# Two pre-activation conv blocks on one core: three engines keep the written plan's order in the front loop and the first convolution

## The chip, the cores and the metric

The program runs on 1 core of a Trainium2 chip. The metric is the device time of one launch in microseconds; before the change it is 4217.51 us, the median of 3 runs (4216.18 to 4220.4). The profiled run has a span of 4215.7 us, and the times below are counted from that span's start.

## The reference, cut to what matters

x is (4, 64, 256, 256) in fp32. `_gn` is a group norm with 32 groups of two channels, without scale. Two layers follow each other:

```python
# layer 0
h = gelu(conv3x3(gn(x), c1_w) + c1_b);  xa, k = split(conv1x1(h, c2_w) + c2_b)
xs = gelu(depthwise 3x1 (depthwise 1x3 (xa)))
mask = top 2 of 3 softmax gate weights of mean(xs)         # over the whole image
y = x + conv1x1(xs + sum_i expert_i(k, xs) * mask_i, proj_w)
# layer 1
h1 = conv3x3(gn(y), q(w1)) + b1;   h1 = relu(batchnorm(h1))  # over all 4 images
h2 = conv3x3(h1, q(w2)) + b2;      out = y + relu(batchnorm(h2) + gn(y))
```

Three things have to be known before work on them can start: the group norm of an image of x before its first convolution, the gate of an image before its experts' output (it needs the last row of xs), and the batch norm of all h1 before the second convolution.

## The kernel before, in words

Partitions hold two times 64 channels: two rows of the image stand side by side, so an image is 128 row pairs of 256 columns. A *group* is two row pairs (512 columns, one PSUM bank); there are 64 of them (NG). A *chunk* is 4 groups (1 MB for DMA); an image has 16 (NCH). A *step* of the front loop does two groups of an image: 32 steps per image (NOCT), 128 for the four images.

The stages are:

- Statistics of image 0 of x: 16 chunks are loaded (stats_load, L268) and run through bn_stats on VectorE (stats_group, L277).
- The front loop (layer 0). Per step it does, on TensorE, the first convolution c in two parts (L396 and L402, matmuls recorded at L328, Gelu on ScalarE L407), the taps a in two parts (L438 and L444; ScalarE L450, two VectorE passes L451 and L454, edge fix L457, Gelu with sum L469), the projection p of two groups (L490), whose result VectorE adds onto x in place (L493), and every second step the expert products k (L476) and q (L506; VectorE L509). After a chunk's last projection SyncE stores it as t1 to DRAM (L495 in the profile). Once an image's gate is known, out_groups adds the experts' part o (L570) to t1, read back by out_load (L559), takes bn_stats of y (L575, L576) and stores y (L581). This runs inside the next image's front loop, 1.25 pairs of groups per step. Inside the front loop of images 0, 1 and 2 stand also the statistics of the next image of x.
- The first convolution of layer 1 (conv1): 65 steps per image. conv1_load (L597) reads a chunk of y, conv1_prepare normalises it on ScalarE (L604), rounds it into the *upper* half tile (ScalarE, L258) and takes the rest as the *lower* half (VectorE, L259). Each group is then 12 matmuls (L247), an eviction by ScalarE (L619) and bn_stats (L624). The out_groups of image 3 run in its first 128 steps.
- A second convolution with the batch norm folded into its input (L768 on), and an output stage that is a stream of loads and stores.

**Buffers.** The ring `in` holds 3 chunks: x of the front loop, later y of conv1. front_load of chunk k therefore waits until chunk k−3 has been stored as t1. The tag `s` holds 2 chunks of the statistics' x (later h1), the tag `o` 3 chunks of y. PSUM has two banks each for c, a and o, one for p and one for k.

**GpSimd** pads the loaded x with the group's mean (front_pad, L363), and writes a one-column *tick* (L321) between the groups of quarter-array matmuls and the full-array matmul that divides them: the next quarter matmuls wait for the tick. A tick queued behind a padding waits for that padding's x.

**What sets the order.** The calls are written into a plan, `plan[step, order]`, and carried out in sorted order (L705 to L707). front_load of chunk k stands at step 2k−1 of its image, order 0. The proj that ends chunk k−3 stands at step 2k−2, order 7. Carrying out the plan doesn't fix the instructions' order on their engines: the framework's scheduler takes the recorded instructions and orders each engine's queue by its own estimate of readiness; an engine then runs its queue in order. Ties in one (step, order) go by insertion.

Of the kernel before, what the change touches and what calls it, by code (L numbers as in the profile page):

```python
# [9 lines left out]
F32 = mybir.dt.float32  # L10
F32R = mybir.dt.float32r
AF = mybir.ActivationFunctionType
ALU = mybir.AluOpType
# [25 lines left out]
CG = 4  # L39
CPAIR = CG * GP  # L40
# [11 lines left out]
def conv_preact_kernel(ctx: ExitStack, tc: tile.TileContext, io, col128, colset, col64):  # L52
    nc = tc.nc
# [36 lines left out]
    def split_tiles(pool, name):  # L90

        tiles = [
            [pool.tile([P, CPAIR + 1, PW], F32R, name=f"half_{name}{i}{j}", bufs=1) for j in range(2)]
            for i in range(2)
        ]
        for t in (*tiles[0], *tiles[1]):
            nc.gpsimd.memset(t.bitcast(F32)[:, :, 0 : PW : PW - 1], 0.0)
        return tiles

    halves = split_tiles(layers.enter_context(tc.tile_pool(name="halves1", bufs=1)), "1")  # L100
# [8 lines left out]
    plan = defaultdict(list)  # L109

    def at(step, order, call, *args):
        plan[step, order].append((call, args))
# [139 lines left out]
                stop=(j == len(terms) - 1),  # L252
            )

    def prepare(halves, y, k, a=0, e=CPAIR + 1):

        upper, lower = (t[:, a:e, 1 : 1 + W] for t in halves[k % 2])
        nc.scalar.activation(upper, y[:, a:e, :], AF.Copy)  # L258
        nc.vector.tensor_tensor(lower, y[:, a:e, :], upper.bitcast(F32), ALU.subtract)  # L259

    gn1, gn2, c1s, c1_bias = {}, {}, {}, {}
    bn1 = const.tile([P, B, 2], F32, name="bn1")
# [329 lines left out]
    y_in, h_out, st_h = {}, {}, {}  # L592
# [4 lines left out]
        nc.sync.dma_start(y[:, a : CPAIR + 1, :], y_d[b][:, k * CPAIR + a - 1 : (k + 1) * CPAIR, :])  # L597

    def conv1_prepare(b, k):
        y = y_in.pop((b, k))  # L600
        a = 1 if k == 0 else 0
        if k == 0:
            nc.gpsimd.memset(y[:, 0, :], 0.0)
        nc.scalar.activation(y[:, a:, :], y[:, a:, :], AF.Identity, bias=gn2[b][:, 2:3], scale=gn2[b][:, 1:2])  # L604
        prepare(halves, y, k)

    def conv1(b, s):

# [43 lines left out]
    def plan_front(b):  # L652
        t = b * F_STEPS
        for k in range(NCH):
            if b > 0 or k >= 2:
                at(t + 2 * k - 1, 0, front_load, b, k)
                at(t + 2 * k - 1, 1, front_pad, b, k)
        for n in range(NOCT):
            at(t + n, 2, front_conv_a, b, n)
            at(t + n, 5, front_conv_b, b, n)  # L660
            at(t + n + 2, 6, front_taps_a, b, n)
            at(t + n + 2, 9, front_taps_b, b, n)
            at(t + n + 3, 3, front_proj, b, n, 0)
            at(t + n + 3, 7, front_proj, b, n, 1)
        for j in range(NG // 4):
            at(t + 2 * j + 3, 4, front_k, b, j)
            at(t + 2 * j + 4, 8, front_q, b, j)
        if b == 0:
            for n in range(3):
                at(n, 3, front_divide, b, n)  # L670
                at(n, 7, front_divide, b, n)
        at(t + NOCT + 2, 1, gate, b)

    def plan_stats(b, t, per):

        for k in range(NCH):
            at(t + int((k - 1) * CG / per), 0, stats_load, b, k, "s", 2)
        for g in range(NG):
            at(t + int(g / per), 10, stats_group, b, g)
        at(t + int(NG / per) + 1, 10, stats_end, b)  # L680

    def plan_out(b, t, per, order):

        for k in range(NCH):
            at(t + int((k - 1.5) * 2 / per) - 1, 0, out_load, b, k)
        for j in range(NG // 2):
            at(t + int(j / per), order, out_groups, b, j)
        at(t + int(NG / 2 / per) + 1, 10, out_end, b)

    def plan_conv1(b):  # L690
        t = CONV1 + b * (NG + 1)
        for k in range(NCH):

            at(CONV1 - 1 + 2 * k if b == 0 and k < 3 else t + 4 * k - 9, 0, conv1_load, b, k)
            at(t + (-1, 2)[k] if b == 0 and k < 2 else t + 4 * k - 4, 1, conv1_prepare, b, k)
        for s in range(NG + 1):
            at(t + s, 2, conv1, b, s)

    for b in range(B):
        plan_front(b)  # L700
        if b < B - 1:
            plan_stats(b + 1, b * F_STEPS + 2, 2.35)
        plan_out(b, (b + 1) * F_STEPS + 3, 1.25 if b < B - 1 else 0.25, 4)
        plan_conv1(b)
    for key in sorted(plan):  # L705
        for call, args in plan[key]:
            call(*args)  # L707


    def bn_affine(mv, gamma, beta, out, name):  # L710
# [16 lines left out]
    def conv2_prepare(i):  # L727
        b, k = chunks[i]
        h = h_in.pop(i)

        cuts = (0, GP + 1, CPAIR + 1) if i == 0 else (0, CPAIR + 1)
        for a, e in zip(cuts, cuts[1:]):
            nc.scalar.activation(h[:, a:e, :], h[:, a:e, :], AF.Relu, bias=ss1[:, 1:2], scale=ss1[:, 0:1])
            if k == 0 and a == 0:
                nc.gpsimd.memset(h[C:P, 0, :], 0.0)
            if k == NCH - 1:
                nc.gpsimd.memset(h[0:C, CPAIR, :], 0.0)
            prepare(halves2, h, k, a, e)
# [62 lines left out]
    for i, (b, k) in enumerate(steps):  # L801
        if i + AHEAD < len(steps):
            end_load(i + AHEAD)
        y, h = y_of.pop(i), h2.pop((b, k))
# [122 lines left out]
```

## Time and profile before

| stretch, us | what | TensorE busy, us | DMA share | GB/s |
|---|---|---|---|---|
| 60 to 89 | weights, start of image 0 | 17.07 of 29 | 0.82 | 251 |
| 89 to 610 | front loop, image 0 | 457.43 of 521 | 0.49 | 151 |
| 610 to 1149 | front loop, image 1 | 517.55 of 539 | 0.48 | 129 |
| 1149 to 1685 | front loop, image 2 | 516.71 of 536 | 0.49 | 130 |
| 1685 to 2220 | front loop, image 3 | 517.27 of 535 | 0.48 | 130 |
| 2220 to 2279 | hand-over to conv1 | 48.29 of 59 | 0.39 | 141 |
| 2279 to 3020 | conv1 | 737.17 of 741 | 0.64 | 228 |
| 3020 to 3750 | second convolution | 720.44 of 730 | 0.48 | 180 |
| 3750 to 4216 | output | 1.18 of 466 | 1.00 | 389 |

The images' limits are the ends of their last Gelu evictions (L407). Over the whole span TensorE is busy 3533.1 us (84%), VectorE 2157.8 us (51%), ScalarE 1667.8 us (40%), GpSimd 58.8 us. A busy time of TensorE counts overlapping quarter-array matmuls once, so it tells where the engine stood still, not how full its array was. A row of a timeline gives start, length, engine (SPq is SyncE issuing DMAs), line, operation, output and inputs, how many were merged into the row, and in brackets the idle time before it and what ended it.

### The profile page before, as it was taken

To read this page: it belongs to the slowest core of one execution; us is meant where nothing else is said; L and a number is where in the kernel's file an instruction comes from. 1 tells how busy PE (TensorE), PEld (TensorE's weight loads), DVE (VectorE), ACT (ScalarE), POOL (GpSimd) and SP (SyncE) were. 2 spreads that over 40 slices of the span, in tenths; PEclk is the share of its full clock that TensorE was granted. 3 is DMA by queue.
4 is the path that set the end of the run, shared out by engine and by line. 5 is a ranking of instruction groups with operands and counts; after the bars stand their busy time and mean duration, and the time that the engine had idled before them with its cause. 6 is when DMAs were issued, how large, how long until landed. Compare 5 with 4: busy or idle time off the path is not lost.

```text
span 4215.7 us, 52658 instructions
## 1 busy us (share of the span) xinstructions
PE 3533.1 (84%) x21596; PEld 1829.6 (43%) x21596; DVE 2157.8 (51%) x2909; ACT 1667.8 (40%) x1962; POOL 58.8 (1%) x359
## 2 busy tenths in 40 slices
PE   3679999999999999999998999999999999950000
PEld 1223333333333332333335777788788888840000
DVE  7753334444444454444545665544444444466566
ACT  0123332222322223322225555666566666642222
POOL 0000000000000000000000000000000000000000
PEclk9889999999999999999999999999999999975555
DMA  9772324554335553354545777555455555349999
GB/s 309 270 222 74 78 78 114 147 147 135 103 104 151 147 154 105 104 144 127 157 128 183 266 260 248 202 201 202 171 202 201 199 204 191 122 163 413 412 412 393
DMA packets 351968, 805.79 MB, mean 191 GB/s; under 512 B 19120, under 2 KB 289456, under 8 KB 289776
## 3 DMA queue, kind: packets, MB, share of 16 engines
q1 hardware_dynamic: 334736, 682.36, 50.2%
q10 hardware_dynamic: 16992, 120.07, 7.2%
q8 instruction: 170, 2.79, 0.3%
q14 instruction: 70, 0.57, 0.0%
HBM read 480.97 MB, written 321.39 MB: 190 GB/s over the span
## 4 chain that ended last, share of the span: by engine, by line
PE 51%; DMA 8%; SPq 4%; DVE 4%; ACT 3%; issue 1%; POOL 0%; ACTq 0%; POOLq 0%; DVEq 0%
PE ps_h L247 30%; PE ps_c L328 10%; DMA y_end<-y_d 4%; PE ps_a L328 4%; PE ps_p L490 3%; SPq L815 3%; PE ps_o L570 2%; DMA yn<-y_d 2%; DMA x<-in_x 1%; SPq L810 1%; PE ps_k L476 1%; DVE half L259 1%; ACT v L806 1%; DVE h L807 1%; ACT half L258 1%; ACT yn L604 1%
## 5 line engine op out<-in xcount | busy, mean ns | idle before, releaser
L247 PE MATMUL ps_h<-half,w_q 128*128 128x512 f32 x6168 | 1450.3, 396 | 6.6 <-ACT half L258 4.7
L247 PEld LDWEIGHTS ps_h<-half,w_q 128*128 128x128 f32 x6168 | 1160.2, 189 | 308.9 <-issue 18.7
L328 PE MATMUL ps_c<-x,c1s 64*64 64x512 f32 x9216 | 1091.6, 607 | 2.0 <-POOL x L363 1.4
L328 PEld LDWEIGHTS ps_c<-x,c1s 64*64 64x64 f32 x9216 | 349.6, 135 | 697.0 <-issue 670.9
L493 DVE TENSOR_TENSOR x<-ps_p,x 128x512 f32<-128x512 f32 x256 | 177.0, 691 | 803.2 <-PE ps_p L490 778.8
L328 PE MATMUL ps_a<-h,av 64*64 64x512 f32 (+1 forms) x3568 | 388.1, 543 | 34.1 <-POOL tick L321 34.0
L490 PE MATMUL ps_p<-xs,m 128*128 128x512 f32 x512 | 296.8, 662 | 70.0 <-ACT xs L469 68.4
L450 ACT ACTIVATE t<-ps_a,tap_bias,m 128x512 f32<-128x512 f32 x256 | 185.1, 773 | 430.4 <-PE ps_a L328 430.4
L407 ACT ACTIVATE h<-ps_c,c1b 128x512 f32<-128x512 f32 x256 | 161.8, 683 | 473.3 <-PE ps_c L328 473.3
L771 DVE BATCH_NORM_STATS2 st_h<-h 128x6 f32<-128x512 f32 x256 | 173.8, 690 | 238.8 <-ACT h L770 238.8
L469 ACT ACTIVATE xs<-t 128x512 f32<-128x512 f32 x256 | 161.2, 630 | 322.6 <-DVE t L457 291.2
L451 DVE SCALAR_TENSOR_TENSOR t<-ps_a,m,t 128x510 f32<-128x510 f32 x256 | 189.9, 743 | 176.2 <-ACT t L450 176.2
L328 PEld LDWEIGHTS ps_a<-h,av 64*64 64x64 f32 x3568 | 140.8, 133 | 300.2 <-issue 198.6
L770 ACT ACTIVATE h<-ps_h,m,scale_w 128x512 f32<-128x512 f32 x256 | 196.9, 769 | 180.5 <-PE ps_h L247 178.6
L619 ACT ACTIVATE h<-ps_h,m,scale_w 128x512 f32<-128x512 f32 x256 | 195.8, 771 | 168.1 <-PE ps_h L247 162.6
L624 DVE BATCH_NORM_STATS2 st_h<-h 128x6 f32<-128x512 f32 x252 | 169.0, 688 | 179.9 <-ACT h L619 179.7
L806 ACT ACTIVATE v<-y_end,shift,gn 128x2048 f32<-128x2048 f32 x64 | 133.8, 2092 | 314.6 <-DMA y_end<-y_d 308.0
L259 DVE TENSOR_TENSOR half<-h,half 128x2304 fp32r<-128x2304 f32 (+1 forms) x65 | 163.8, 2520 | 147.8 <-ACT half L258 147.8
L259 DVE TENSOR_TENSOR half<-yn,half 128x2304 fp32r<-128x2304 f32 x64 | 163.7, 2558 | 134.3 <-ACT half L258 134.1
L807 DVE SCALAR_TENSOR_TENSOR h<-h,ss,v 128x2048 f32<-128x2048 f32 x64 | 150.3, 2350 | 153.7 <-ACT v L806 150.7
L575 DVE SCALAR_TENSOR_TENSOR y<-ps_o,ob,y 128x512 f32<-128x512 f32 x256 | 186.7, 741 | 60.7 <-PE ps_o L570 60.7
L277 DVE BATCH_NORM_STATS2 st_x<-xs_in 128x6 f32<-128x512 f32 x256 | 159.9, 680 | 75.8 <-DMA xs_in<-in_x 75.3
(150 smaller groups left out, 2037.6 us busy)
## 6 DMA issues: line engine op xcount, KB each, us to landing
h_d<-h ACTq DMA_DIRECT2D x114, 1024.0 KB, 4.1
h<-h_d SPq DMA_DIRECT2D x64, 1152.0 KB, 5.2
yn<-y_d SPq DMA_DIRECT2D x60, 1152.0 KB, 5.5
xs_in<-in_x SPq DMA_DIRECT2D x64, 1024.0 KB, 5.0
t_d<-x SPq DMA_DIRECT2D x64, 1024.0 KB, 4.8
y<-t_d SPq DMA_DIRECT2D x64, 1024.0 KB, 6.0
y_d<-y SPq DMA_DIRECT2D x256, 256.0 KB, 4.0
y_end<-y_d SPq DMA_DIRECT2D x64, 1024.0 KB, 11.4
```

The costliest lines, as they stand in the source:

```text
L247: nc.tensor.matmul(ps[:, 0:n, :], w[:, kx, m, :], t[:, i + m : i + m + n, kx : kx + W], start=(j == 0), stop=(j == len(terms) - 1),)
L259: nc.vector.tensor_tensor(lower, y[:, a:e, :], upper.bitcast(F32), ALU.subtract)
L328: ins = nc.tensor.matmul(ps[o, at_out[0] : at_out[1], :], w[i], rhs[i], **flags)
L450: nc.scalar.activation(flat(t), flat(ps), AF.Identity, bias=tap_bias, scale=sh[:, 1:2])
L451: nc.vector.scalar_tensor_tensor(t[:, :, 1:W], ps[:, :, 0 : W - 1], sh[:, 0:1], t[:, :, 1:W], ALU.mult, ALU.add)
L490: divide(nc.tensor.matmul(flat(ps), c128("proj"), xss[b, g], start=True, stop=True))
L493: nc.vector.tensor_tensor(t1, ps, t1, ALU.add)
L575: nc.vector.scalar_tensor_tensor(y, ps, out_bias[b], y, ALU.add, ALU.add)
L619: nc.scalar.activation(h, ps, AF.Identity, bias=c128("b1"), scale=w_scale["w1"])
L770: nc.scalar.activation(o, ps, AF.Identity, bias=c128("b2"), scale=w_scale["w2"])
L806: nc.scalar.activation(v, y, AF.Identity, bias=shift[:, b : b + 1], scale=gn2[b][:, 1:2])
L807: nc.vector.scalar_tensor_tensor(h, h, ss2[:, 0:1], v, ALU.mult, ALU.add)
```

## The change

The plan's calls are carried out inside a manual schedule for three engines: SyncE (SP), VectorE (DVE) and GpSimd (Pool) keep the order in which the plan records their instructions. TensorE and ScalarE are still ordered by the scheduler. Since the plan's order now counts, some places in it are changed:

- front_pad goes from order 1 to order 6 of its step.
- stats_load goes from order 0 to order 11, the end of its step.
- out_load goes from order 0 to order 5, and starts at most two steps ahead of its stage.
- conv1's preparation is divided: normalising and the upper half (ScalarE) stay at order 1, the lower half (VectorE) goes to order 10.

It is for having each queue's order follow from the plan and not from the scheduler's estimate. No instruction is added or removed.

```diff
-    def prepare(halves, y, k, a=0, e=CPAIR + 1):
+    def prepare(halves, y, k, a=0, e=CPAIR + 1, do=("upper", "lower")):
         upper, lower = (t[:, a:e, 1 : 1 + W] for t in halves[k % 2])
-        nc.scalar.activation(upper, y[:, a:e, :], AF.Copy)
-        nc.vector.tensor_tensor(lower, y[:, a:e, :], upper.bitcast(F32), ALU.subtract)
+        if "upper" in do:
+            nc.scalar.activation(upper, y[:, a:e, :], AF.Copy)
+        if "lower" in do:
+            nc.vector.tensor_tensor(lower, y[:, a:e, :], upper.bitcast(F32), ALU.subtract)
...
     def conv1_prepare(b, k):
-        y = y_in.pop((b, k))
+        y = y_in[b, k]
...
-        prepare(halves, y, k)
+        prepare(halves, y, k, do=("upper",))
+
+    def conv1_lower(b, k):
+        prepare(halves, y_in.pop((b, k)), k, do=("lower",))
...
-                at(t + 2 * k - 1, 1, front_pad, b, k)
+                at(t + 2 * k - 1, 6, front_pad, b, k)
...
-            at(t + int((k - 1) * CG / per), 0, stats_load, b, k, "s", 2)
+            at(t + int((k - 1) * CG / per), 11, stats_load, b, k, "s", 2)
...
-            at(t + int((k - 1.5) * 2 / per) - 1, 0, out_load, b, k)
+            at(max(t + int((k - 1.5) * 2 / per) - 1, t - 2), 5, out_load, b, k)
...
             at(t + (-1, 2)[k] if b == 0 and k < 2 else t + 4 * k - 4, 1, conv1_prepare, b, k)
+            at(t + (-1, 2)[k] if b == 0 and k < 2 else t + 4 * k - 4, 10, conv1_lower, b, k)
...
-    for key in sorted(plan):
-        for call, args in plan[key]:
-            call(*args)
+
+    with tc.manual_schedule(
+        engines={mybir.EngineType.SP, mybir.EngineType.DVE, mybir.EngineType.Pool}
+    ):
+        for key in sorted(plan):
+            for call, args in plan[key]:
+                call(*args)
```

## The prediction

> **What bounds the kernel now.** I read the page's slices first, for the stage in which TensorE is not full.
>
> ```profile
> PE   3679999999999999999998999999999999950000
> DVE  7753334444444454444545665544444444466566
> DMA  9772324554335553354545777555455555349999
> GB/s 309 270 222 74 78 78 114 147 147 135 103 104 151 147 154 105 104 144 127 157 128 183 266 260 248 202 201 202 171 202 201 199 204 191 122 163 413 412 412 393
> ```
>
> A slice is 105 us. TensorE (PE) is full from slice 5 to slice 35, except in slices 1 to 3; there the DMA and VectorE (DVE) rows are at their front-loop highest. The last four slices are a DMA-bound tail that the change does not touch. So the stage to look at is the first image of the front loop. The table of windows gives it in numbers (columns: window, its length, then busy time and count of PE, PEld, DVE, ACT, POOL, granted clock, DMA share, GB/s):
>
> ```profile
> 130.00:272.00 142.00, 97.31 (x680) 29.93 (x680) 99.42 (x172) 26.19 (x50) 1.79 (x14) 0.82 0.78 268
> 330.00:562.00 232.00, 232.00 (x1906) 75.80 (x1902) 79.27 (x138) 73.71 (x140) 5.90 (x41) 1.00 0.32 80
> ```
>
> Same image, same work per step: 680 matmuls in 142 us against 1906 in 232 us, that is 4.8 and 8.2 per us. Who is waited for between 60 and 330 us stands in the table of waits (total, times, longest):
>
> ```profile
> DVE st_x L277 <- DMA xs_in<-in_x: 67.4, 25, 9.1
> ACT xs L469 <- DVE t L457: 71.3, 16, 10.2
> PE ps_p L490 <- ACT xs L469: 59.1, 8, 15.9
> POOL x L363 <- DMA x<-in_x: 54.7, 4, 16.2
> ```
>
> The chain is legible: VectorE sits in a bn_stats of the *next* images until its chunk lands, ScalarE waits for VectorE's t, TensorE waits for ScalarE. And the padding waits for the image's own x. SyncE's timeline says why x is late:
>
> ```profile
> 107.15 65.41 SPq L270 DMA_DIRECT2D xs_in<-in_x  x17
> 176.14 0.39 SPq L495 DMA_DIRECT2D t_d<-x  x1
> 177.35 0.34 SPq L270 DMA_DIRECT2D xs_in<-in_x  x1
> 181.41 2.61 SPq L355 DMA_DIRECT2D x<-in_x  x4
> ```
>
> The scheduler has put 17 statistics loads ahead of the first t1 store; all 48 MB of images 1 to 3 go through here.
>
> From the ends of the Gelu evictions (L407, trace) I take step lengths. Undisturbed, steps of image 0 alternate 12.7 and 15.6 us (k's matmuls in every second one). Steps 3 to 10 took 31.6, 21.4, 25.6, 21.7, 25.5, 21.9, 25.5, 18.5: against 15.6, 12.7, ... an excess of 78 us.
>
> Images 1 to 3 (539, 536, 535 us) lose time at single chunks of x:
>
> ```profile
> 1299.32 0.34 SPq L559 DMA_DIRECT2D y<-t_d  x1
> 1299.76 0.38 SPq L495 DMA_DIRECT2D t_d<-x  x1
> 1308.07 2.62 SPq L355 DMA_DIRECT2D x<-in_x  x4
> 1316.63 0.34 POOL L363 TENSOR_SCALAR x<-zeros,gn 128x20 f32<-128x20 f32 x1 [11.93 <-DMA x<-in_x]
> 1317.05 1.09 PE L328 MATMUL ps_a<-h,av 64*64 64x512 f32 x8 [3.12 <-POOL tick L321]
> 1317.96 7.03 PE L328 MATMUL ps_c<-x,c1s 64*64 64x512 f32 x48
> ```
>
> The chunk's buffer comes free when the t1 store lands. A y load 0.44 us ahead of it doubled that, to 8.2 us; x then lands 8.4 us after its first issue, the tick stands behind the padding on GpSimd, and TensorE stops 3.1 us. Such stalls cost 18 us in image 1, 15 in image 2 and 15 in image 3 (chunks 5, 9 and 13, some 5 us each).
>
> **What the skill says.** "TensorE: Matmul & The Clock Gate", section "Architectural detail": ACT and DVE are strict FIFO. The trace agrees: with bn_stats ahead, t waits up to 18.8 us for nothing of its own. "DMA: Bandwidth & Descriptors", section "Queues, rings and completion order": a queue's descriptors are consumed in ring order. The trace agrees: loads issued *behind* x leave it at 8.5 us (first issue 181.4, landed 189.9; undisturbed 8.4), and one ahead of the store costs 4 us. The clock-gate page, section "What's actually happening", has the array fall to half clock after an idle window of about 3.4 us; here the 48 matmuls after the 3.12 us gap took 7.03 us, 5.33 elsewhere, so I add up to 1.7 us to long stalls.
>
> **The change part by part.** The order of the built program tells what moves.
>
> *SyncE, image 0.* The 48 stats loads spread over images 0 to 2, one per 1.7 steps. Nothing then holds x or t: −78 us. That takes the steady part (232 of 232 us busy) as the pace, with its DMA at 80 GB/s and 32%: a stats load per 1.7 steps, about 25 us, adds 42 GB/s.
>
> *VectorE.* Each step gains 2 or 3 bn_stats of 0.68 us after t. In that place VectorE was idle 2.16 us before x (L493); three take 2.0. Hidden. Loads are issued one to two steps (13 to 30 us) ahead and land in 4.7 to 12 us, so no wait on arrival.
>
> *SyncE, the new waits.* In each of images 0 to 2, six stats loads stand between a t1 store and its x load (chunks 5, 6, 7, 11, 12, 13). For 7 and 13 the buffer is free: the load goes out at once behind the store; at 222.1 the same sequence left the store at 5.2 and x at 8.9 us. Cost 0. For 5, 6, 11 and 12 the buffer is freed by a bn_stats of the same step, executed after the t's: they end 5.3 us after the store's issue, plus 0.7. So SyncE holds until +6.2, x is issued at +6.9 instead of +4.5, and lands behind 1 MB in the ring (+0.8, estimated from pieces landing 1.25 us apart). Padding is done at +16.6; image 0 tolerates +14.6 (chunk 8: store 390.0, matmul 405.6, less 1.0 for the taps behind the tick). Late by 2.0, with some cold clock 2.8: 4 × 2.8 = +11 us in image 0. If every such wait were absorbed: 0; if all six paid 4 us: 24.
>
> *Images 1 to 3, y loads.* y chunks 6 and 11, and the next image's first, move away from the store of chunks 5, 9 and 13. In image 3, with no stats loads, all three stalls go: −14. In images 1 and 2 chunk 5 keeps half (late 1.2 + 1.5 instead of 5), 9 and 13 go (−4.5, −5), chunk 11 (tolerates +15.9) becomes late by 0.7 and costs 2, chunk 6 0.5: −9 each.
>
> *End of statistics.* In program order bn_aggr (1.86 us) comes after the step's t's, so TensorE's first small matmul, now after 18 records of c instead of before them, waits until about 6.3 us into the step; the scheduler had it early and hidden. Partly that replaces waits of 1.4 and 1.2 us. Estimate +2.5 for an x chain, +1.5 for a y chain: 3 × 2.5 + 3 × 1.5 = +12 (0 to 22).
>
> *Padding later.* GpSimd's built order differs by one instruction (chunk 2 of image 0). Cost 0: that padding's data is needed 50 us later.
>
> *First convolution.* There TensorE is busy 737 of 741 us, so nothing is to be gained. lower at the step's end: the upper copy ends 3.0 us into a chunk's last-but-four step, bn_stats and a y pair (2.9) end by 5.1, lower (2.56) by 7.7, needed at 11.2 (4 steps of 2.8). Hidden. Only the hand-over changes: lower of chunk 1 now stands behind the whole gate on VectorE. By hand from the trace (gate's last op 8 us after ps_g, then bn_stats, two x, low, lower: 6 us) TensorE stands about 12 us with four matmuls begun, but saves the 9.08 us that it waited for xs at 2236.6; chunk 2 then waits about 4 more: +7 (−3 to +20).
>
> Sum: −78 + 11 − 18 − 14 + 12 + 7 = −80; 4217.5 − 80 = 4138.
>
> **Rivals.** (a) *Everything absorbed*: no new stall, chain or hand-over cost, all stalls of images 1 to 3 gone (18 + 15 + 15): −126, 4091. For: ring slack of 6 to 7 us at half the chunks of images 1 to 3; against: 1.1 us in image 0. (b) *VectorE's order binds the first convolution*: lower misses its 11.2 us at the 32 chunks beside y work by 2 us: +64, 4202. Against: 3.5 us of margin; for: VectorE is 55% busy there and a late h shifts all behind it. (c) *SyncE's order becomes the bound*: a stats load that waits for VectorE holds the next t1 store or x load at every chunk, not at four. 48 chunks × 3.7 (2.0 + 1.7 cold) = 178, of which about 16 is counted: 4138 + 162 = 4300, slower. For: SyncE issues everything in one order and the slack is only 2 us; against: loads of odd steps stand *behind* x. (d) *The 78 us come back elsewhere*: the same 48 MB compete in images 0 to 2 and slow t1 and x by 1.7 us per chunk: 48 × 1.7 = 80, 4218, no change.
>
> **How the numbers follow.** Forecast 0.73 (4138, spread about 4105 to 4170), a 0.07, b 0.08, c 0.08, d 0.04. Faster: forecast, a, b = 0.88; same 0.04; slower 0.08. The range 4103 to 4195 takes in the unknown costs (new stalls 0 to 24 in image 0, chains 0 to 22, hand-over −3 to +20) and leaves out c, d, a and the far part of b.
>
> **What would show it.** Right: slices 1 to 3 at 9 on the PE row and near 100 GB/s, image 0 about 455 us long, a wait SPq L270 <- DVE st_x of some us at four chunks per image, stalls behind the tick at image 0's chunks 5, 6, 11 and 12, and no long PE gap at 2236. Wrong: tick waits at most chunks (c), waits of ps_h for lower in steady chunks (b), or image 0 short and images 1 and 2 longer by as much (d).

## The result, and the profile after

The changed kernel takes 4144.74 us (median of 4 runs, 4140.64 to 4146.6) against 4216.85 us for the kernel before beside it (4215.34 to 4220.4): a ratio of 0.9826, 95% interval 0.9809 to 0.9844. The profiled executions, 4144.1 and 4215.7 us, differ by 71.6 us; all the accounts below are of these two. The forecast was 4138 us, range 4103 to 4195: faster, as the result is, and 6.7 us too low.

The slices of the page, of the kernel after (one slice is 103.6 us), in the rows that were shown of before:

```profile
PE   3999999999899999999999999999999999950000
DVE  5434445656366564555546566444444444465656
DMA  7334446665366663455536776655455555359999
GB/s 233 100 103 116 107 120 182 182 182 156 95 183 186 193 168 94 127 147 153 141 95 239 256 256 239 224 202 196 183 194 201 202 200 196 113 183 412 412 413 394
```

TensorE is at 8 or 9 from slice 1 to slice 35: the dip to 6 and 7 in slices 1 and 2 is gone. In slices 1 to 3 the DMA moves 100, 103 and 116 GB/s where it moved 270, 222 and 74: the 48 MB of statistics chunks are spread. The table of windows of the kernel after, over the two stretches that were shown of before (window, length, busy time and count of PE, PEld, DVE, ACT, POOL, granted clock, DMA share, GB/s):

```profile
130.00:272.00 142.00, 136.38 (x1066) 43.42 (x1058) 59.64 (x101) 40.92 (x78) 3.12 (x23) 0.95 0.42 118
330.00:562.00 232.00, 221.06 (x1734) 71.75 (x1726) 96.61 (x167) 70.40 (x131) 7.23 (x39) 0.96 0.37 96
```

1066 matmuls in the first 142 us instead of 680: that is what was won. But the second stretch has 1734 instead of 1906 and is no longer full: something new stands there, and the end of image 0 (554 us, before 610) now lies in it too. The table of waits of TensorE between 60 and 2150 us of the kernel after names it (total, times, longest):

```profile
PE ps_a L330 <- POOL tick L323: 24.7, 15, 2.9
PE ps_m_x L222 <- DVE mv_x L238: 11.0, 3, 3.7
PE ps_m_y L222 <- DVE mv_y L238: 10.7, 3, 3.6
```

The 59 us of ps_p <- xs are gone. The tick's waits are the x loads that come late; the two ps_m rows, which were not there before, are the ends of the statistics. On SyncE the forecast's new wait, L272 <- st_x, is there too: 8 waits between 89 and 560 us, 129.6 us in all, 65.7 of it in one at the start.

From the ends of the Gelu evictions I take step lengths again and put each excess to its cause. "Stalls" are excesses at single chunks of x; the last row before the sum is what the other rows leave over.

| term of the forecast | forecast, us | measured, us |
|---|---|---|
| steps 3 to 10 of image 0 come down to 12.7 and 15.6 | −78 | −81 |
| new waits of SyncE, image 0 (chunks 5, 6, 7, 11, 12, 13) | +11 | +24.2 (5.8, 5.8, 0.6, 4.6, 5.9, 1.5) |
| stalls of images 1 to 3, old ones gone less new ones | −32 | −36.0 (−10.5, −11.2, −14.3) |
| ends of statistics | +12 | +20.1 (2.7, 9.3, 7.1, 1.0 in images 0 to 3) |
| hand-over and first convolution | +7 | +5.1 |
| start, single steps, tail | 0 | −4.0 |
| sum | −80 | −71.6 |

Here is chunk 5 of image 0 in the kernel after. First SyncE's timeline: t1 store, statistics load, x load.

```profile
194.78 0.38 SPq L497 DMA_DIRECT2D t_d<-x  x1
200.91 0.33 SPq L272 DMA_DIRECT2D xs_in<-in_x  x1
201.33 2.68 SPq L357 DMA_DIRECT2D x<-in_x  x4
```

The store lands at 199.6; SyncE holds the statistics load until 200.91, when a bn_stats has freed its buffer, and x goes out 6.5 us after the store (forecast 6.9). It lands at 211.7, 10.4 us after its first issue (forecast 9.3), and the padding is done 17.5 us after the store (forecast 16.6, tolerated 14.6). Then TensorE's timeline, at this chunk and at the undisturbed chunk 8:

```profile
212.41 1.98 PE L330 MATMUL ps_a<-h,av 64*64 64x512 f32 x8 [2.83 <-POOL tick L323]
214.17 7.39 PE L330 MATMUL ps_c<-x,c1s 64*64 64x512 f32 x48
...
306.67 1.09 PE L330 MATMUL ps_a<-h,av 64*64 64x512 f32 x8
307.58 5.33 PE L330 MATMUL ps_c<-x,c1s 64*64 64x512 f32 x48
```

TensorE stands 2.83 us, and the same 56 matmuls behind the gap take 2.95 us longer than at chunk 8 (0.89 + 2.06). Behind the gap TensorE runs cold, that is at half its granted clock, and here that costs as much as the wait itself.

An end of statistics, image 0, in the timelines of VectorE (first line) and TensorE of the kernel after:

```profile
535.78 1.88 DVE L238 BATCH_NORM_AGGREGATE mv_x<-st_x 128x2 f32<-128x384 f32 x1
...
531.40 2.74 PE L330 MATMUL ps_c<-x,c1s 64*64 64x512 f32 x18
537.80 0.56 PE L222 MATMUL ps_m_x<-mv_x,m 128*128 128x1 f32 x2 [3.66 <-DVE mv_x L238]
538.29 1.98 PE L330 MATMUL ps_c<-x,c1s 64*64 64x512 f32 x8
540.20 0.58 PE L230 MATMUL ps_v_x<-d_x,m 128*128 128x1 f32 x2
540.72 2.83 PE L330 MATMUL ps_c<-x,c1s 64*64 64x512 f32 x12
```

bn_aggr stands behind the step's t's; TensorE waits 3.66 us for it, and then again runs cold: 8 matmuls in 1.98 us, as many as take 1.09 warm (chunk 8 above), and 12 in 2.83, which take 1.93 at full clock in a kernel further down (bn_aggr ahead). With the small matmuls between them that is about 2.2 us more.

### The profile page after: what moved, and what is told of

Same layout as the page of the kernel before. It is cut to its first block, busy times and chain, and to the rows that moved or that the text cites. A ratio compares the mean times of both kernels' runs of the same rounds, so it can differ in the third digit from the quotient of the medians.

```text
span 4144.1 us, 52631 instructions
## 1 busy us (share of the span) xinstructions
PE 3522.8 (85%) x21596; PEld 1826.3 (44%) x21596; DVE 2186.9 (53%) x2909; ACT 1669.2 (40%) x1962; POOL 59.1 (1%) x359
## 4 chain that ended last, share of the span: by engine, by line
PE 75%; DMA 11%; DVE 6%; SPq 5%; ACT 2%; issue 1%; POOL 0%; POOLq 0%; ACTq 0%; DVEq 0%
PE ps_h L247 34%; PE ps_c L330 21%; PE ps_a L330 7%; PE ps_p L492 6%; DMA y_end<-y_d 4%; DMA x<-in_x 4%; PE ps_o L572 3%; SPq L825 2%; PE ps_k L478 2%; PE ps_q L508 1%; DMA t_d<-x 1%; DMA out<-h 1%; SPq L820 1%; DVE h L817 1%; SPq L357 1%
## 5 line engine op out<-in xcount | busy, mean ns | idle before, releaser
L330 PE MATMUL ps_a<-h,av 64*64 64x512 f32 (+1 forms) x3568 | 386.6, 540 | 24.8 <-POOL tick L323 24.7
L453 DVE SCALAR_TENSOR_TENSOR t<-ps_a,m,t 128x510 f32<-128x510 f32 x256 | 190.9, 746 | 213.2 <-ACT t L452 213.2
L456 DVE SCALAR_TENSOR_TENSOR t<-ps_a,m,t 128x510 f32<-128x510 f32 x256 | 191.7, 749 | 9.0
L578 DVE BATCH_NORM_STATS2 st_y<-y 128x6 f32<-128x512 f32 x256 | 177.8, 695 | 8.9
```

The costliest lines, as they stand in the source:

```text
L330: ins = nc.tensor.matmul(ps[o, at_out[0] : at_out[1], :], w[i], rhs[i], **flags)
L453: nc.vector.scalar_tensor_tensor(t[:, :, 1:W], ps[:, :, 0 : W - 1], sh[:, 0:1], t[:, :, 1:W], ALU.mult, ALU.add)
L456: nc.vector.scalar_tensor_tensor(t[:, :, 0 : W - 1], ps[:, :, 1:W], sh[:, 2:3], t[:, :, 0 : W - 1], ALU.mult, ALU.add)
L578: nc.vector.bn_stats(st_y[b][:, g, :], y)
```

## Experiments: which kept order it takes

Only the set of engines that keep the plan's order is changed.

```diff
-        engines={mybir.EngineType.SP, mybir.EngineType.DVE, mybir.EngineType.Pool}
+        engines={mybir.EngineType.SP}
```

> SyncE's queue alone keeps the plan's order; VectorE and GpSimd are ordered by the scheduler again. Theory (the queue's order is what freed image 0: with the 48 stats loads spread, no bn_stats can hold VectorE for long, whoever orders it): the steps 3 to 10 of image 0 are about 116 us together as in the changed kernel (before: 192), and the time is within 15 us of the changed kernel, 4130 to 4160 us. Rival (VectorE's order is needed, because the scheduler puts a bn_stats ahead of the step's t wherever it thinks the chunk has landed): waits of DVE bn_stats for loads come back and image 0 keeps 20 us or more of its excess, 4165 us or more.

Measured: 4219.51 us, ratio to the kernel before 1.0014 (1.0005 to 1.0022). The whole gain is gone, though not where the rival put it: image 0 lasts 455.6 us, shorter than in the changed kernel (466.4), and steps 3 to 10 are 113 us. Image 3 (518.5 against 521.7) and the hand-over with the first convolution (794.6 against 807.0) are shorter too. But images 1 and 2 grow to 586.8 and 577.0 us (538.2 and 530.6 in the changed kernel). The waits of VectorE, then of TensorE, of this kernel between 546 and 1710 us, which is images 1 and 2:

```profile
DVE st_x L279 <- DMA xs_in<-in_x: 149.8, 29, 10.8
...
PE ps_p L492 <- ACT xs L471: 39.2, 13, 7.7
PE ps_o L572 <- DVE y L577: 28.1, 16, 8.4
```

The scheduler puts bn_stats ahead of work that TensorE needs, and VectorE waits in it for a chunk that isn't there: up to 10.8 us. In image 0 it does that too (13 waits, 77.2 us in all) and TensorE hardly feels it; in images 1 and 2, where VectorE also has the y pairs, it does. There the trace has 27 gaps of TensorE of over 0.7 us, 93 us in all. Six are ends of statistics; each of the other 21, 85 us, has such a wait of VectorE less than 8 us ahead of it or beside it. Half clock behind the gaps costs another 51 us; in these images of the changed kernel it costs 15. The theory that SyncE's order is enough falls: spreading the loads over images 0 to 2 spreads the waits with them, unless VectorE's order puts bn_stats where its chunk has landed. The outcome is that of the forecast's rival (d), 78 us that come back elsewhere; the way is another, for (d) had t1 and x slowed by the traffic, and here it is VectorE's order.

```diff
-        engines={mybir.EngineType.SP, mybir.EngineType.DVE, mybir.EngineType.Pool}
+        engines={mybir.EngineType.DVE}
```

> VectorE alone keeps the plan's order; SyncE's queue is ordered by the scheduler. Theory (the two-buffer statistics tag can't run ahead of a VectorE that reads its chunks in the plan's order, so the loads are spread whoever orders the queue): image 0 loses its 78 us of excess here too, steps 3 to 10 about 116 us, and the time is 4130 to 4160 us; with y loads standing next to the t1 stores again, stalls of some 5 us at x chunks 5 and 9 of images 1 to 3 come back, which is up to 25 us of that. Rival (the queue's order is what matters): stats loads stand ahead of t1 stores and x loads again, image 0 is 500 us or longer, 4185 us or more.

Measured: 4201.26 us, ratio 0.9970 (0.9959 to 0.9981). Image 0 does as the theory says (459.2 us, steps 3 to 10 at 117 us): with VectorE in order the two-buffer tag spreads the loads by itself. But images 1 to 3 last 560.2, 560.0 and 537.7 us, together 67 us more than in the changed kernel, where the theory allowed 25; the time itself lies where the rival had it, above 4185. SyncE's timeline of this kernel at chunk 5 of image 0:

```profile
195.85 0.37 SPq L497 DMA_DIRECT2D t_d<-x  x1
201.18 0.60 SPq L357 DMA_DIRECT2D x<-in_x  x1
201.97 0.46 SPq L272 DMA_DIRECT2D xs_in<-in_x  x1
202.49 1.93 SPq L357 DMA_DIRECT2D x<-in_x  x3
```

The scheduler slips statistics loads between the four pieces of x; and in images 1 to 3 y loads stand 0.4 us ahead of t1 stores again (at chunk 5 of image 1 the store then lands after 9.3 us). Here the last piece of this x lands 13.2 us after the first was issued (214.4), against 8.4 undisturbed. In TensorE's waits of this kernel between 60 and 2150 us, the tick's row, 24.7 us in the changed kernel, has become

```profile
PE ps_a L330 <- POOL tick L323: 65.6, 22, 6.8
```

So SyncE alone gives nothing, VectorE alone 0.3%, both (with GpSimd) 1.7%. The two do different things: VectorE's order keeps bn_stats from holding the engine, SyncE's keeps the loads out of the way of t1 and x. GpSimd is not what the two kernels lack: in their traces its paddings and ticks follow each other as in the changed kernel, but for one padding of image 0.

For GpSimd the question is the padding's place.

```diff
-                at(t + 2 * k - 1, 6, front_pad, b, k)
+                at(t + 2 * k - 1, 1, front_pad, b, k)
```

> The changed kernel with the padding back at its old place in the step, which with GpSimd in the plan's order is one tick earlier. Theory (the place is needed for the kept order: the padding of a chunk then holds a tick for x; by the trace the tick at 298.5 us of the changed kernel would wait for the x that lands at 304.8, and TensorE has about 2 us to spare): each of 61 chunks costs some 4.5 us of wait and 1.7 us of cold clock, about +380 us, 4520 us (4350 to 4600). Rival (the tick has slack of a whole half step, so one place more or less costs nothing): within 10 us of 4145.

Measured: 4443.93 us, ratio 1.0537 (1.0520 to 1.0555): 300 us slower than the changed kernel. The timelines of GpSimd and TensorE of this kernel at one of the 61 chunks:

```profile
151.68 0.34 POOL L365 TENSOR_SCALAR x<-zeros,gn 128x20 f32<-128x20 f32 x1 [14.74 <-DMA x<-in_x]
151.94 0.10 POOL L323 MEMSET tick<- 128x1 f32 x1
...
152.10 5.15 PE L330 MATMUL ps_c<-x,c1s 64*64 64x512 f32 x24 [4.30 <-POOL tick L323]
```

One place earlier, and the padding waits 14.74 us for x with a tick behind it, for which TensorE stands 4.30 us and then takes 5.15 us for 24 matmuls (2.81 when warm). The theory is right in kind and 80 us too high in size (51 waits of ps_c for the tick in the front loop, not 61). The kernel before had its paddings behind that tick too, all but one as in the changed kernel, though the plan had them ahead of it; so against that kernel the later place costs nothing, as forecast. Once GpSimd keeps the plan's order, it is needed.

## Experiments: what the new stalls are

Four kernels change what stands around t1 store and x load. The first moves the statistics loads of even steps out from between them.

```diff
-            at(t + int((k - 1) * CG / per), 11, stats_load, b, k, "s", 2)
+            s = t + int((k - 1) * CG / per)
+            at(*((s, 11) if s % 2 else (s + 1, 0.5)), stats_load, b, k, "s", 2)
```

> The changed kernel, but the stats loads of even steps stand behind the next step's x loads instead of between a t1 store and its x load. Theory (the x load pays for the stats load ahead of it, by SyncE's wait for bn_stats and by its 1 MB in the ring): the six stalls of image 0 (24 us) and those at x chunks 5, 6 and 11 of images 1 and 2 (6 to 8 us) go, image 0 lasts about 442 us, the time is 4112 to 4120 us. Rival (the stalls come from the DMA traffic of 48 MB, wherever it is issued): the stalls move to other chunks, the time stays within 5 us of the changed kernel's 4145.

Measured: 4116.28 us, ratio 0.9768 (0.9753 to 0.9783). All six stalls of image 0 are gone (its steps are 12.7 and 15.6 throughout) and it lasts 441.8 us; images 1 and 2 fall by 6.1 and 1.6 us. The stalls were those loads, and not the traffic as such: the same 48 MB still go through in the same three images. SyncE's order of this kernel at the same chunk:

```profile
195.50 0.38 SPq L497 DMA_DIRECT2D t_d<-x  x1
200.86 2.60 SPq L357 DMA_DIRECT2D x<-in_x  x4
203.55 0.55 SPq L272 DMA_DIRECT2D xs_in<-in_x  x1
```

Is it SyncE's wait, or the 1 MB ahead of x? The next kernel keeps the order and frees the buffer.

```diff
-            at(t + int((k - 1) * CG / per), 11, stats_load, b, k, "s", 2)
+            at(t + int((k - 1) * CG / per), 11, stats_load, b, k, "s", 3)
```

(and 3 for 2 at the tag's two other uses.)

> The changed kernel with three buffers instead of two for the statistics chunks; SyncE's order is unchanged, so a stats load still stands between t1 store and x load at the same chunks, but its buffer is free and SyncE doesn't wait for bn_stats. Theory (three quarters of the stall is the wait): chunks 5, 6, 11 and 12 of image 0 cost what 7 and 13 cost now (0.6 and 1.5 us): the six stalls of image 0 fall from 24 to about 6 us, those of images 1 and 2 by half; the time is about 4145 - 20 = 4125 us. Rival (the 1 MB in the ring ahead of x is what costs, whoever waits): image 0's stalls stay above 15 us, 4137 us or more.

Measured: 4128.23 us, ratio 0.9790 (0.9776 to 0.9805). SyncE's timeline of this kernel, chunk 5 of image 0:

```profile
194.68 0.38 SPq L497 DMA_DIRECT2D t_d<-x  x1
195.11 2.22 SPq L272 DMA_DIRECT2D xs_in<-in_x  x1
200.20 2.59 SPq L357 DMA_DIRECT2D x<-in_x  x4
```

The load goes out at once, x 1.0 us earlier than in the changed kernel; the store ahead lands at 5.5 instead of 4.8, x 8.5 us after its issue. Image 0's stalls come to 8.8 us (chunk 5: none, 6: 1.2, 7: 1.4, 8: 0.1, 11: 0.5, 12: 1.2, 13: 4.4). So about 15 of the 24 us go with the wait, and some 9 stay with the load's place in the queue: at chunks 6, 7, 11, 12 and 13 x still lands 9.9, 10.1, 9.5, 9.4 and 11.4 us after its first issue, and the latest is the one with the 4.4 us. The result lies between the theory (6 us) and the rival (over 15), nearer to the theory.

The next puts the load at the beginning of its step.

```diff
-            at(t + int((k - 1) * CG / per), 11, stats_load, b, k, "s", 2)
+            at(t + int((k - 1) * CG / per), 0, stats_load, b, k, "s", 2)
```

> The changed kernel with the statistics loads back at the beginning of their step instead of its end, in the plan's order. Theory (a load at the step's beginning waits for a bn_stats that VectorE reaches only at the step's end; in even steps SyncE then holds the t1 store that comes in the middle, so store and x are late by about 4 us more than in the changed kernel, at the same four chunks 5, 6, 11 and 12 of images 0 to 2): these steps last some 22 to 25 instead of 18 us in image 0, the time rises by 40 to 70 us, to 4185 to 4215 us. Rival (a load issued at the step's beginning has landed before the store goes out and costs nothing, as the loads behind x): the stalls go, 4115 to 4125 us.

Measured: 4280.35 us, ratio 1.0155 (1.0140 to 1.0170): slower than the kernel before, and beyond the theory's 4185 to 4215. SyncE's timeline of this kernel at chunk 5:

```profile
200.75 0.33 SPq L272 DMA_DIRECT2D xs_in<-in_x  x1
201.13 0.43 SPq L497 DMA_DIRECT2D t_d<-x  x1
209.55 2.59 SPq L357 DMA_DIRECT2D x<-in_x  x4
```

Now the wait for bn_stats holds the store itself, and the store, with 1 MB just issued ahead of it, takes 8.4 us to land. TensorE's waits for the tick (60 to 2150 us) in this kernel:

```profile
PE ps_a L330 <- POOL tick L323: 130.5, 19, 11.9
```

Image 0 does what the theory says: its four chunks last 23.0, 24.4, 24.2 and 23.3 us. Images 1 and 2 were priced too low: there the steps of chunks 3 and 9 lengthen too, and those of 5, 6, 11 and 12 last up to 28.4 us (590.9 and 590.5 us for the images).

The last of the four is the y load next to the store.

```diff
-            at(max(t + int((k - 1.5) * 2 / per) - 1, t - 2), 5, out_load, b, k)
+            s = max(t + int((k - 1.5) * 2 / per) - 1, t - 2)
+            at(*((s - 1, 5.5) if b < B - 1 and k in (6, 11) else (s, 5)), out_load, b, k)
```

> The changed kernel with the y loads of chunks 6 and 11 of images 0 to 2 moved one step earlier, so that they stand just ahead of a t1 store again. Theory (a y load that has just been issued makes the store behind it land at 8 instead of 4.5 us, so x's buffer comes free late): stalls of some 5 us at x chunks 5 and 9 come back in images 1 to 3, +25 us (4170 us). Rival (the stalls of the kernel before came from the order of VectorE, and went with that): 4145 us, no step of images 1 to 3 longer by over 1 us.

Measured: 4172.83 us, ratio 0.9892 (0.9878 to 0.9907), 28 us above the changed kernel. In images 1 to 3 the steps of chunk 5 last 19.7, 19.0 and 19.1 us (15.8, 15.8, 13.8 in the changed kernel) and those of chunk 9 last 19.4, 20.3 and 18.2 (13.8): +28.9 us at just these six steps. SyncE's timeline of this kernel, image 1, chunk 5:

```profile
702.84 0.33 SPq L561 DMA_DIRECT2D y<-t_d  x1
703.26 0.38 SPq L497 DMA_DIRECT2D t_d<-x  x1
707.76 0.33 SPq L272 DMA_DIRECT2D xs_in<-in_x  x1
712.72 2.62 SPq L357 DMA_DIRECT2D x<-in_x  x4
```

x leaves 9.5 us after the store, against 6.6 at this chunk in the changed kernel; in the kernel before it was 9.5 here and 8.3 at the same chunk of image 2 (1299.76). The forecast's reading of those stalls is confirmed. It is not every store that matters: in the changed kernel a y load still stands 0.4 us ahead of the stores that free the buffers of chunks 6 and 10 of images 1 and 2. There x leaves 8.3 to 9.4 us after the store, and the steps lose at most 0.9 us. These chunks have the room that chunks 5 and 9 lack.

## Experiments: the ends of statistics, and the hand-over

In addition to the loads behind x, bn_aggr is split off and put ahead of the last step's t's (its order is 3.5 instead of 10; the same for x and y).

```diff
+        at(t + int(NG / per) + 1, 3.5, aggregate, st_x, b, f"x{b}")
         at(t + int(NG / per) + 1, 10, stats_end, b)
...
+        at(t + int(NG / 2 / per) + 1, 3.5, aggregate, st_y, b, f"y{b}")
         at(t + int(NG / 2 / per) + 1, 10, out_end, b)
```

> As the kernel with the stats loads behind x, and in addition bn_aggr stands ahead of the t's in the last step of each statistics pass, so that TensorE's group-mean matmul no longer waits for it behind two t's. Theory (end of statistics costs what the waits of ps_m_x and ps_m_y show, 11.0 and 10.7 us, seven waits): both waits go to under 2 us in all and the time falls by 10 to 20 us against the kernel with the loads behind x alone, to about 4100 us. Rival (the chain behind it, several small operations between VectorE, TensorE and GpSimd in turn, sets the length, and only its start moves; 1.86 us of bn_aggr ahead of t costs the c matmuls as much): a change of under 5 us.

Measured: 4101.34 us, ratio 0.9735 (0.9720 to 0.9749), 15 us below the kernel with only the loads moved. TensorE's timeline of this kernel at the end of image 0:

```profile
508.55 0.38 PE L222 MATMUL ps_m_x<-mv_x,m 128*128 128x1 f32 x2
508.86 2.79 PE L331 MATMUL ps_c<-x,c1s 64*64 64x512 f32 x18
513.84 0.38 PE L230 MATMUL ps_v_x<-d_x,m 128*128 128x1 f32 x2 [2.20 <-DVE d_x L228]
514.15 1.93 PE L331 MATMUL ps_c<-x,c1s 64*64 64x512 f32 x12
```

The first small matmul no longer waits. The chain behind it now does, 2.20 us at its second matmul (ps_v_x and ps_v_y wait 10.6 and 6.9 us in all), so the waits shrink and don't vanish; the 12 matmuls behind the 2.20 us are warm. The last steps of the images, which is what counts, are 3.0, 6.5, 3.8 and 2.7 us shorter: 16 of the 20 us that the ends had cost.

The hand-over: the lower half of the first convolution back behind the upper.

```diff
-            at(t + (-1, 2)[k] if b == 0 and k < 2 else t + 4 * k - 4, 10, conv1_lower, b, k)
+            at(t + (-1, 2)[k] if b == 0 and k < 2 else t + 4 * k - 4, 1, conv1_lower, b, k)
```

> The changed kernel with the first convolution's lower half back at its old place, just behind the upper half. Theory (the place at the step's end costs nothing in the steady first convolution, and a few us at the hand-over, where lower stands behind the gate): first convolution and hand-over together, 804 us in the changed kernel, change by -5 to +2 us; 4140 to 4147 us. Rival (VectorE in strict order, lower then stands ahead of the x adds and y pairs and waits for ScalarE's upper copy, 3.0 us into the step, with bn_stats and y pairs behind it): +1 us or more at each of the 64 chunks, 4200 us or more.

Measured: 4134.74 us, ratio 0.9807 (0.9792 to 0.9822). From image 3's last Gelu to the first matmul of the next statistics (ps_m_bn) it is 803.3 us here, 807.0 in the changed kernel and 801.9 before. The 3.7 us less are as expected. The median is 10 us below that of the changed kernel, and so just below the expected 4140 to 4147; the profiled executions differ by 5.1 us (4139.0 and 4144.1). This is where the time lies in the changed kernel, by TensorE's timeline:

```profile
2187.05 2.07 PE L572 MATMUL ps_o<-low,wm 32*128 32x512 f32 x2 [4.68 <-DVE wm L552]
2195.03 11.89 PE L247 MATMUL ps_h<-half,w_q 128*128 128x512 f32 x44 [1.91 <-DVE half L261]
```

and in the kernel with lower earlier:

```profile
2144.96 1.60 PE L492 MATMUL ps_p<-xs,m 128*128 128x512 f32 x2 [3.49 <-DVE x L495]
...
2203.23 2.08 PE L247 MATMUL ps_h<-half,w_q 128*128 128x512 f32 x4 [7.56 <-ACT half L259]
```

Either way TensorE stands some us: for the gate's weights and a lower half in the one, for an x add and an upper half in the other. In the steady convolution neither place costs: beyond the hand-over the longest wait for a half is 0.96 us in the changed kernel (1.3 us in two), and none is left with lower earlier.

Last, the three edits together (loads behind x, bn_aggr ahead, lower behind upper):

> Three of the edits tried singly, together: stats loads of even steps behind x, bn_aggr ahead of the last t's, lower half of the first convolution just behind the upper. Theory (they act at different places: chunks 5 to 13, the ends of statistics, the hand-over): the first two gave 4101 us together, the third about -4 in the hand-over (799.7 against 803 to 804 us): 4097 us. Rival (lower's earlier place lengthens the hand-over once the chain before it is shorter): 4101 us or more.

Measured: 4094.64 us (4093.14 to 4100.34), ratio 0.9719 (0.9703 to 0.9736). This is faster than the kernel before by 2.8% and than the changed kernel by about 1.1% (0.9719 / 0.9826). Its interval overlaps that of the kernel without the third edit (0.9735), so the third edit's own gain isn't settled by the times; the hand-over went from 807.7 to 802.1 us in the profiles.

## Why the prediction came out as it did

The forecast of 4138 us was 6.7 us too low, and that it came so near owes something to luck: the two costs of the new order came out 21 us higher than priced, and the other rows of the table together 13 us lower.

**Removal: right.** −81 against −78; the difference is step 3, which the working counted as 15.6 us and which lasts 13.0 undisturbed. The undisturbed steps with three bn_stats in them are still 12.7 and 15.6 us, so these are hidden as worked out, and slices 1 to 3 carry 100 to 116 GB/s. (Of these three the working says that TensorE is not full in the kernel before; that is so in 1 and 2 alone, slice 3 was at 9 with 74 GB/s.) What the working did not say is that this needs both queues: it priced SyncE's spread at −78 and VectorE's order at nothing. The runs show that with SyncE's order alone image 0 is 65 us shorter than before and images 1 and 2 are 88 us longer. VectorE is strictly FIFO, as the Trainium skill has it ("TensorE: Matmul & The Clock Gate", section "Architectural detail"), and a bn_stats put too early holds everything behind it, up to 10.8 us here.

**New waits of SyncE in image 0: mechanism right, price half of what it cost.** The four chunks named are the four that stall, and 7 and 13 nearly don't (0.6 and 1.5 us, not 0). Each of the four was priced at 2.8 us, late by 2.0 and 0.8 for cold clock; chunk 5 measured 2.83 and 2.95. Two terms were short. The x load behind 1 MB took 10.4 us to land, not 9.3. And the cold clock was taken from one gap of the kernel before, where it cost 1.7 us, scaled down. Over image 0 the tick's waits are 13.2 us, and half clock costs 10.6 us: 2.9 to 3.0 at chunks 5, 6 and 12 and 1.7 at chunk 11. Together that is nearly all of the 24.2.

**Images 1 to 3: right**, −36 against −32, image by image within 2.2 us. Moving two y loads per image back brings the stalls of chunks 5 and 9 back.

**Ends of statistics: mechanism right, size 20 instead of 12.** The term of +2.5 per x chain and +1.5 per y chain left the cold clock out. Over these steps (the last of image 0, the last two of images 1 to 3) TensorE's idle time grew by 9.6 us from the kernel before to the changed one, which the term had covered, and what half clock costs there by 9.2 us, from 3.4 to 12.6. Putting bn_aggr ahead took back 16 of the 20.

**Hand-over: size right, makeup in part.** +5.1 against +7. The working had TensorE stand about 12 us with four matmuls begun, save the 9.08 us of the wait for xs and lose some 4 us at chunk 2. In the changed kernel the convolution does stand 12.7 us there, but six matmuls of o and p fill 6.1 of them, and TensorE's idle time is 6.6 (the 4.68 and 1.91 above). It waits 1.60 us for xs and 1.01 at chunk 2. From the last Gelu to ps_m_bn TensorE's idle time is 16.8 us against 16.5 before; its busy time is 4.7 us longer, of which half clock accounts for 1.3. What the other 3.4 are stays open, so that this term came near is luck in part. Lower at the step's end is hidden but for 1.3 us.

**Padding later: right** that it costs nothing against before: in the traces GpSimd's order differs from before by one padding, as the working had it.

**The rivals.** (a), everything absorbed, is what the loads behind x come near to (4116, 4101 with bn_aggr ahead, 4095 with lower earlier): the slack was there, but not for a load in that one place. (c), SyncE's order as the bound, did not come. With the loads at the beginning of the step the time came near its 4300 (4280), but from stalls of up to 14.6 us at four to six chunks of an image and not from 3.7 us at each, so the nearness of the number is chance; the forecast was right to rest (c) on *where* in the step the load stands. (d) has its outcome in SyncE's order alone, by another way. (b), lower as the bound of the first convolution, is excluded by the same steady convolution with either place.

GpSimd's kept order alone, SyncE and VectorE without it, and the y loads at the beginning of their step were not tried.

## What to carry to other kernels

When one hand-written order feeds another, try both together: a queue's order decides where data waits, the consumer's decides who waits for data. Here SyncE's order alone moved the loss instead of removing it, and VectorE's alone left most of it. In a queue that issues in strict order, look at what stands between a store and the load that reuses its buffer; a transfer that itself waits for a buffer belongs behind that load, not ahead of it. And when pricing a stall of TensorE of nearly 3 us or more, add the slow matmuls behind it, which here cost 1.7 us or about 3; from 2 us on they can come too.

## What was unexpected of the hardware

A gap of TensorE of about 3 us costs up to double, and its length does not tell the price. The gap of 2.83 us in the changed kernel cost 2.95 us of slow matmuls, the longer one of the kernel before, 3.12 us at 1317.05, only 1.7. The windows around the two, the changed kernel first, give the granted clock in the column before the last two:

```profile
211.50:218.30 6.80, 5.89 (x28) 1.78 (x32) 2.90 (x5) 2.17 (x4) 0.37 (x2) 0.50 0.01 2
...
1318.05:1321.40 3.35, 3.35 (x24) 0.98 (x20) 2.32 (x5) 1.44 (x2) 0.00 (x0) 0.50 0.00 0
```

In the trace's record of the granted clock the first spell at half lasts 6.83 us, from 211.49 on, and the second 3.41 us, from 1318.02 on. The cost is half of what TensorE is busy in the spell: half of 5.9 us and half of 3.4. Over the twelve profiles, of 248 spells that begin before 3000 us, 106 last 3.41 us, 100 last 6.83, and the rest 10.24, 13.65 or 17.07, all whole multiples of the first.

Whether a spell comes at all is not settled by length either, for short gaps. After the 2.20 us above the 12 matmuls were warm and took 1.93 us. In the kernel with the three edits together the same place has

```profile
513.20 0.38 PE L230 MATMUL ps_v_x<-d_x,m 128*128 128x1 f32 x2 [2.19 <-DVE d_x L228]
513.51 2.51 PE L331 MATMUL ps_c<-x,c1s 64*64 64x512 f32 x12
```

and a spell of 3.41 us from 514.74 on. Of gaps that were met at full clock and stand alone (none of 0.6 us or more in the 14 us before or 7 us behind), a spell began in or within 2.5 us behind 3 of 29 from 1.4 to 2.0 us long, 25 of 30 from 2.0 to 2.8, and 191 of 192 longer ones, over all twelve profiles before 3600 us. The Trainium skill ("TensorE: Matmul & The Clock Gate", section "What's actually happening") has the array fall to half clock after an idle window of about 3.4 us and return after a busy one of that length; the spells here agree with that length and its multiples, but gaps of 2.0 to 2.8 us, which lie below it, were mostly followed by one.

A transfer issued about 0.4 us ahead in the same queue delays the store behind it by some 4 us: the 1 MB t1 store lands in 4.4 us alone and in 8.4 behind a statistics load. "DMA: Bandwidth & Descriptors", section "Queues, rings and completion order", says that descriptors are consumed in ring order; the trace agrees. In the other order, with the load 0.4 us behind it, the store loses only about 0.8 us (5.23 at 263.03 of the changed kernel, 4.43 at 291.95 without).
